# The last demodulation of a composed convolution moves from the weights to the rows that leave PSUM, and ScalarE makes the composition's first operand

## The chip, the core and the metric

The kernel runs on one core of a Trainium2 chip. The metric is the device time of one launch in microseconds (us): the median over runs. Below, PE is TensorE (matrix products), DVE is VectorE, ACT is ScalarE, POOL is GpSimd and SP is SyncE, whose queue issues most of the transfers. PSUM is the memory that TensorE writes its products to; SBUF is the working memory.

## The reference, cut to what matters

The input x has 32 samples of 64 channels and 1024 positions; every sample also has a condition vector of 128 numbers, its style. Two layers follow one another, and each adds its result to x:

```python
out = x
for l, typ in enumerate(('same', 'upsample', 'same', 'downsample')):
    s = style @ mod_w[l].T + mod_b[l]
    weight = SCALE * w[l] * s[:, None, :, None]
    demod = rsqrt(sum(weight * weight, axis=(2, 3)) + 1e-8)
    weight = weight * demod[:, :, None, None]     # one kernel per sample
    out = conv(out, weight, typ) + b[l]            # with a blur for up and down
...
x = x + ffn0(conv0(x))      # 64 experts of rank 16, the 16 best scores gated by softmax
x = x + ffn1(conv1(x))      # int4 weights, 1024 x 1024, and a bias
```

The two ffn parts act on the 1024 positions of one channel, so a row (sample, channel) is what they call a token. The demodulation of the fourth convolution is one number for each sample and output channel, that is, one number for each token.

## The kernel before

**Composition.** The four convolutions of a sample are linear and have no activation between them, so the kernel doesn't run them one by one. It runs the first convolution, and it multiplies the other three (with the blurs and strides) together into one small set of tap matrices for each sample, which TensorE then applies once to the first convolution's output. The work goes by pairs of samples: 16 pairs p in each of the layers i = 0 and 1, and a pair's 2 x 64 rows are the 128 partitions of everything that comes after.

- `composed1(i, p)` builds the operand `r` (L586): the fourth convolution's weights `w3p`, times a per-sample column `al2`, times the row of the fourth demodulation, `tbl[i, p][:, h, 0]`, broadcast over the partitions. One VectorE instruction for each of the two samples. TensorE multiplies `r` with `tw` into the product `g` (L596), and ScalarE takes it out of PSUM with a per-partition scale as `gs` (L608). There is one buffer for `r`.
- `composed2` makes `f` (L619) from `gs`, and `weights` copies it out (L634, L636, L637) and adds (POOL, L642, L648, L652): these are the tap matrices of `w(k)`.
- `first` is the first convolution (`c`, L757 or L768 and L773; ScalarE's copy out L758, or `yt` L770 and VectorE's L774 with a pointer scale). `differences_of` forms differences of its outputs (VectorE L716, POOL L722 and L730).
- `rest` applies the composed taps: products `r` in PSUM (L834, L843 or L852, L875), VectorE's sums (L865, L866, L883, L884), and in pairs that use nine products one more, `p`: ScalarE first copies the constant row of the fourth layer, `tbl[i, p][:, h, 1]`, into a PSUM bank (L822), TensorE adds `p` on it (L826), ScalarE copies it out as `rt` (L830). The result is then split into a high part (L149, `thx`) and a low part (L919, `tlx`) for the ffn products.
- `tbl` holds two rows a sample: row 0 is the demodulation, row 1 the constant that the biases make. `last_rows` makes them from two transposes per layer (L345, ScalarE's L346); for the first two pairs `spread_rows` broadcasts them by small matmuls (L355, copied by ScalarE in L364), for all others a DMA reads them from `rowd` (L571).
- `ends` computes the edge rows of all samples apart from the taps, layer by layer, with `scaled` (L464, L466), L482 and L483, L519 to L521, and products `ue`, `ve`, `re`.

**The ffn of layer 0.** `layer0` is its first half: score and expert products `h` (L955) in three chunks; `joined` takes them out of PSUM as `hs`. Pairs 0 and 1 (`WHOLE`) do it by a plain copy (L974). The others sum two banks: ScalarE scales the first (L976), VectorE adds the scaled second (L977). Then come the gates (L987 to L997, with ScalarE's `ga` L993), and POOL's gating (L1003). The gated rows are stored for all pairs; the second half, after the last pair, transposes them (`ht`, L1079) and forms the products `o` (L955), added to x in L1123 and L1124; meanwhile the factors of layer 1 (`factors`, L331 to L334 among them) and its first pairs are prepared.

**The ffn of layer 1** (`layer1`): products `q` (L1204) in three chunks; a column of `q` becomes `nrs` (L1223), VectorE forms `sc` from `q` and the weight scales (L1228) and adds with `nrs` (L1226), POOL adds it up (L1230). POOL also prepares the next pair's `o` with the bias (L1187, 128 x 1024).

**What sets the order.** Loop k of layer 0 handles pair k's ffn and, between its products, the next pairs' convolutions: `later(k + 1)` is `rest`, `conv(k + 2)` is `first`, `compose(k + 2)` is `composed1`, `weights(k + 2)` is `composed2`. The program records them in this order and a scheduler then arranges the instructions of each engine; every engine works its own list in order, and waits where an operand or a buffer is not ready. PSUM has eight banks: three for `c` and `r`, one for `g`, `f`, `p` and the small products, four for the ffn.

Of the kernel before, what the change touches and what calls it, by code (L numbers as in the profile page):

```python
# [15 lines left out]
P = 128  # L16
# [47 lines left out]
def adaln_ffn_kernel(ctx: ExitStack, tc: tile.TileContext, t, out: bass.AP):  # L64
# [44 lines left out]
    styp = const.tile([P, NP], F32, name="styp")  # L109
    rows = const.tile([B, 2, C], F32, name="rows")  # L110
    re = const.tile([P, 2, 2, P], F32, name="re")
# [6 lines left out]
    hgd = dram.tile([NP, P, L], F32, name="hgd")  # L118
    rowd = dram.tile([2, B, 2, C], F32, name="rowd")
    red = dram.tile([2, NP, 2, 2, 2, C], F32, name="red")  # L120
# [53 lines left out]
    def factors(i, *rooms):  # L174
# [20 lines left out]
        bi = tmp(NL)  # L195
        sty, dem, al, be = (tmp(NL, B) for _ in range(4))
        for h, hs in enumerate(halves):
# [78 lines left out]
        with tc.issue_after(done["positions"].ins if i == 0 else copied.ins):  # L276
            root = nc.scalar.activation(dem, dpv, AF.Sqrt, bias=eps, scale=0.5)
        v = nc.vector.reciprocal(dem, dem)
        with tc.issue_after(v.ins):
# [7 lines left out]
        with tc.issue_after(root.ins):  # L287
# [3 lines left out]
            nc.scalar.copy(tw[C:, 0, 1], w2v[C:, 0, C:])  # L291
        last_rows(i, 0, dem[:, 3])
        yield
# [16 lines left out]
        nc.vector.tensor_copy(al[:, 3], dem[:, 3])  # L310
        nc.vector.tensor_copy(be[:, 3], bib(3))
        nc.vector.tensor_copy(al2, al[:, 2])
# [15 lines left out]
        for l, src in ((2, be[:, 1]), (3, tm)):  # L328
            ps = mpst(f"cs{i}_{l}")[:, :B]
            for k in range(KT):  # L330
                nc.tensor.matmul(ps, cw[:, l, k], src, start=(k == 0), stop=(k == KT - 1))  # L331
            dst = tm if l == 2 else cst
            nc.vector.scalar_tensor_tensor(dst, ps, 8.0, al[:, l], ALU.mult, ALU.mult)
            nc.vector.tensor_tensor(dst, dst, be[:, l], ALU.add)  # L334
            if l == 2:
                yield
        last_rows(i, 1, cst)
        nc.sync.dma_start(rowd[i], rows)
        yield

    def last_rows(i, k, v):


        ps = mpst(f"rows{i}_{k}")
        nc.tensor.transpose(ps[:B, :C], v[:C], ident[:C, :C])  # L345
        nc.scalar.copy(rows[:, k], ps[:B, :C])  # L346
        if i == 0:
            spread_rows(0, k)

    def spread_rows(p, k):  # L350

        ps = fpst(f"rows{k}_{p}")[:, :P].rearrange("p (n c) -> p n c", n=2)
        for h in range(2):
            n = 2 * p + h
            nc.tensor.matmul(  # L355
                ps[:, h],
                ident[:B, n : n + 1].to_broadcast([B, P]),
                rows[:, k],
                start=True,
                stop=True,  # L360
            )
        if k == 0:
            tbl[0, p] = wk.tile([P, 2, 2, C], F32, tag="tbl", name=f"tbl0_{p}", bufs=3)
        nc.scalar.copy(tbl[0, p][:, :, k], ps)  # L364

# [83 lines left out]
    def ends(i, lo, hi, room, behind=()):  # L449
# [11 lines left out]
        def scaled(dst, ps, l):  # L461
            a = alp[:, l, lo:hi].unsqueeze(2).to_broadcast([P, n, dst.shape[2]])
            b = bep[:, l, lo:hi].unsqueeze(2).to_broadcast([P, n, dst.shape[2]])
            nc.vector.tensor_tensor(dst, ps, a, ALU.mult)  # L464
            by = nc.vector if l in (0, NL - 1) else eng
            done[f"s{l}"] = by.tensor_tensor(dst, dst, b, ALU.add)  # L466

# [101 lines left out]
    def tables(i, p):  # L569
        v = tbl[i, p] = wk.tile([P, 2, 2, C], F32, tag="tbl", name=f"tbl{i}_{p}", bufs=3)  # L570
        nc.sync.dma_start(  # L571
            v.rearrange("p a b c -> p (a b c)"),
            rowd[i, 2 * p : 2 * p + 2].rearrange("a b c -> (a b c)").partition_broadcast(P),
        )
# [6 lines left out]
    def composed1(i, p):  # L581

        r = wk.tile([P, 2, 2, C], F32, tag="r3", name=f"r3_{i}_{p}", bufs=1)
        for h in range(2):
            n = 2 * p + h
            nc.vector.scalar_tensor_tensor(  # L586
                r[:, :, h],
                w3p,
                al2[:, n : n + 1],
                tbl[i, p][:, h, 0].unsqueeze(1).to_broadcast([P, 2, C]),  # L590
                ALU.mult,
                ALU.mult,
            )
        ps = (fpst if i == 1 and p > 2 else mpst)(f"g{i}_{p}")
        for k in range(2):
            nc.tensor.matmul(  # L596
                ps[:, k * P : (k + 2) * P],
                tw[:, k].rearrange("p a b -> p (a b)"),
                r.rearrange("p a b c -> p (a b c)"),
                start=(k == 0),  # L600
                stop=(k == 1),
                skip_group_check=True,
            )
        g = wk.tile([P, 3, 2, C], F32, tag="g", name=f"gs{i}_{p}", bufs=1)
        v = ps[:, : 3 * P].rearrange("p (k h c) -> p k h c", k=3, h=2)
        for h in range(2):
            n = 2 * p + h
            nc.scalar.activation(g[:, :, h], v[:, :, h], AF.Copy, scale=al1[:, n : n + 1])  # L608
        return g
# [170 lines left out]
    def rest(i, n, y, f):  # L780
# [19 lines left out]
        if whole:  # L800
            yb, yo = y
            ps = cpst(f"r{i}_{n}")
            for j in range(4):
                for k in range(4):
# [8 lines left out]
                    )  # L813
            c = tbl[i, p][:, h, 1].unsqueeze(1).to_broadcast([P, 2 * 4, C])
            done["r0"] = nc.vector.tensor_tensor(th, shape(ps), c, ALU.add)
# [3 lines left out]
        if nine(i, p):  # L819
# [3 lines left out]
                pt.rearrange("p (q c) -> p q c", q=2),  # L823
                tbl[i, p][:, h, 1].unsqueeze(1).to_broadcast([P, 2, C]),
            )
# [36 lines left out]
        else:  # L862
            parts = [v.rearrange("p (q c) -> p q c", c=C) for v in (m, ps[:, 2 * P :])]
            common = tbl[i, p][:, h, 1].unsqueeze(1).to_broadcast([P, 4, C])
        done["m"] = nc.vector.tensor_tensor(*parts, common, ALU.add)  # L865
# [99 lines left out]
    def layer0(p, ws):  # L965
# [5 lines left out]
        def joined(col, w, qd):  # L971
            dst = hs[:, col : col + w]
            if whole:
                nc.scalar.copy(dst, qd[0])  # L974
                return
            nc.scalar.activation(dst, qd[0], AF.Copy, scale=1.0 + 1.0 / RADIX)  # L976
            nc.vector.scalar_tensor_tensor(dst, qd[1], -1.0 / RADIX, dst, ALU.mult, ALU.add)  # L977

# [215 lines left out]
    def layer1(p, wq, aux):  # L1194


        o = residual.pop(p)
        for c in range(3):
            if c == 0:
# [21 lines left out]
            if c == 0:  # L1221
                nrs = tiny.tile([P, 1], F32, tag="nrs", name=f"nrs{p}")
                nc.vector.tensor_scalar_mul(nrs, ps[:, 0:1], -1.0)  # L1223
            if c == (0 if p == NP - 1 else 2):
                with tc.issue_after(done["lo"].ins):
                    nc.vector.scalar_tensor_tensor(o, aux[:, 1], nrs, o, ALU.mult, ALU.add)  # L1226
            s = wk.tile([P, QC], F32, tag="yt", name=f"sc{p}_{c}", bufs=2)[:, : QC - a]
            nc.vector.tensor_tensor(s, ps[:, a:], aux[:, 0, cs], ALU.mult)  # L1228
            eng = nc.vector if p == NP - 1 and c == 2 else nc.gpsimd
# [101 lines left out]
    run(set0)  # L1331
    spread_rows(1, 0)
    for h in range(2):
# [4 lines left out]
    for h in range(2):  # L1338
        later(0, h)
    spread_rows(1, 1)  # L1340
    weights(1)
# [202 lines left out]
```

## Time and profile before

| | before |
|---|---|
| median of 3 runs | 893.91 us |
| lowest and highest | 893.53 and 894.51 us |
| span of the profiled execution | 893.1 us |
| PE busy | 866.1 us, 97% |
| DVE busy | 723.2 us, 81% |
| POOL busy | 531.1 us, 59% |
| ACT busy | 352.4 us, 39% |
| DMA | 109.81 MB, mean 123 GB/s |

The profile is one execution. Its span reaches from its first to its last instruction; the runs are timed around the launch, which is some 0.8 us more. In order of time: the start, then the taps and the products `h` of layer 0 for all 16 pairs (the last `h` at 397 us), then its products `o` (428.6 to 621.5), then the pairs of layer 1 (`q` from 621.9 to the end). A busy engine is not by that alone the one that sets the time: what matters is which engine the others wait for, and where.

### The profile page before, as it was taken

The numbers are of one execution on the slowest core, as the hardware profiler recorded it, in microseconds if no ns is written. First come the engines' busy times: TensorE is split into PE (matmuls) and PEld (weight loads), VectorE is DVE, ScalarE is ACT, GpSimd is POOL, SyncE is SP. The second block draws the span as 40 slices with busy tenths as digits, with TensorE's granted clock in tenths as the row PEclk, the third lists the DMA queues.
The fourth block names the chain that finished last, engine by engine and source line by source line (L and its number), as shares of the span: only waits on it lengthen the run. The fifth ranks groups of instructions, "written<-read, shape, count | busy, mean of one in ns | idle before, by whom it ended". The sixth has DMA issues, their size and how long they took to land.

```text
span 893.1 us, 14916 instructions
## 1 busy us (share of the span) xinstructions
PE 866.1 (97%) x5033; PEld 775.1 (87%) x5033; DVE 723.2 (81%) x1460; ACT 352.4 (39%) x817; POOL 531.1 (59%) x745
## 2 busy tenths in 40 slices
PE   6989999999999999999999999999999999999997
PEld 4876888999999999994688888888899999999997
DVE  4475898888888888778986765669999999999996
ACT  6444544444444444333332221247333433343340
POOL 7235654666666666556572222343787888888884
PEclk9999999999999999999999999999999999999999
DMA  8632222222232222345475666555543334334321
GB/s 240 155 73 54 54 69 62 88 89 80 79 91 83 81 79 71 106 178 149 139 232 193 201 193 197 189 192 167 164 117 111 98 100 143 114 90 139 122 66 71
DMA packets 49739, 109.81 MB, mean 123 GB/s; under 512 B 13700, under 2 KB 22400, under 8 KB 49664
## 3 DMA queue, kind: packets, MB, share of 16 engines
q1 hardware_dynamic: 48704, 107.88, 39.5%
q10 hardware_dynamic: 960, 0.99, 0.5%
q8 instruction: 40, 0.66, 0.3%
q14 instruction: 35, 0.29, 0.1%
HBM read 70.97 MB, written 37.88 MB: 122 GB/s over the span
## 4 chain that ended last, share of the span: by engine, by line
PE 42%; DVE 7%; POOL 2%; issue 2%; ACT 0%; DVEq 0%; POOLq 0%; ACTq 0%
PE o L955 16%; PE q L1204 11%; PE f L619 3%; PE r L875 3%; PE c L773 2%; PE r L834 1%; PE r L843 1%; PE c L768 1%; PE ht L1079 1%; PE g L596 1%; DVE cv L716 1%; DVE x L1124 1%; PE p L826 1%; DVE rt L866 1%; DVE r L884 0%
## 5 line engine op out<-in xcount | busy, mean ns | idle before, releaser
L716 DVE TENSOR_TENSOR cv<-cv 128x257 f32<-128x257 f32 x120 | 105.8, 913 | 1.3 <-ACT cv L758 0.9
L730 POOL TENSOR_TENSOR cv<-cv 128x256 f32<-128x256 f32 x120 | 77.7, 647 | 29.8 <-DVE cv L716 25.1
L722 POOL TENSOR_TENSOR cv<-cv 128x128 f32<-128x128 f32 x100 | 39.0, 411 | 67.5 <-PE r L843 48.3
L1204 PE MATMUL q<-wq,thx 128*128 128x342 f32 x384 | 73.0, 332 | 2.1 <-ACT thx L913 2.1
L955 PE MATMUL h<-wa,tdx 128*128 128x352 f32 (+1 forms) x336 | 72.2, 351 | 0.2 <-DVE wa L382 0.2
L1204 PE MATMUL q<-wq,tlx 128*128 128x342 f32 x384 | 72.3, 330 | 0.0
L619 PE MATMUL f<-gs,iw 128*128 128x128 f32 (+1 forms) x384 | 68.2, 327 | 0.1
L619 PEld LDWEIGHTS f<-gs,iw 128*128 128x128 f32 x384 | 61.8, 190 | 5.9 <-issue 0.5
L955 PE MATMUL h<-wa,thx 128*128 128x352 f32 (+1 forms) x336 | 64.7, 333 | 0.0
L1204 PEld LDWEIGHTS q<-wq,thx 128*128 128x128 f32 x384 | 60.3, 189 | 4.1 <-ACT thx L913 3.2
L770 ACT ACTIVATE yt<-c,be,al 128x257 f32<-128x257 f32 x56 | 31.7, 567 | 80.4 <-PE c L768 77.3
L875 PE MATMUL r<-cv 128*128 128x128 f32 x480 | 63.4, 274 | 0.0
L1204 PEld LDWEIGHTS q<-wq,tlx 128*128 128x128 f32 x384 | 61.9, 189 | 0.8
L955 PE MATMUL h<-wa,tlx 128*128 128x352 f32 (+1 forms) x336 | 62.4, 327 | 0.0
L955 PE MATMUL o<-wb,thh 128*128 128x512 f32 x224 | 60.4, 402 | 1.5 <-ACT wb L375 1.5
L935 POOL TENSOR_TENSOR tdx<-thx,tlx 128x1024 fp32r<-128x1024 f32 x14 | 34.7, 2479 | 44.5 <-ACT tlx L927 36.2
L955 PEld LDWEIGHTS h<-wa,tdx 128*128 128x128 f32 x336 | 56.9, 188 | 2.4 <-DVE wa L382 0.5
L1123 DVE SCALAR_TENSOR_TENSOR cv<-o,cv 128x512 f32<-128x512 f32 x26 | 18.0, 692 | 50.2 <-PE o L955 50.2
L955 PE MATMUL o<-wb,tlh 128*128 128x512 f32 x224 | 58.4, 397 | 0.0
L875 PEld LDWEIGHTS r<-cv 128*128 128x128 f32 x480 | 58.4, 191 | 0.0
L634 ACT COPY cv<-f 128x256 f32<-128x256 f32 x64 | 24.0, 375 | 83.9 <-PE f L619 46.3
L642 POOL TENSOR_TENSOR cv<-cv 128x256 f32<-128x256 f32 x60 | 50.0, 833 | 11.4 <-ACT cv L637 11.4
(313 smaller groups left out, 2274.6 us busy)
## 6 DMA issues: line engine op xcount, KB each, us to landing
cv<-in_x_dram SPq DMA_DIRECT2D x60, 256.0 KB
cv<-x1e SPq DMA_DIRECT2D x64, 192.5 KB
x1e<-dd SPq DMA_DIRECT2D x16, 514.0 KB
hgd<-hs SPq DMA_DIRECT2D x16, 512.0 KB
hg<-hgd SPq DMA_DIRECT2D x16, 512.0 KB
x1d<-x SPq DMA_DIRECT2D x16, 512.0 KB
xb<-x1d SPq DMA_DIRECT2D x16, 512.0 KB
out_dram<-o SPq DMA_DIRECT2D x15, 512.0 KB
```

Source lines behind the costliest of these rows:

```text
L619: done["f"] = nc.tensor.matmul(pv[:, n : n + 2 - k], iw[:, e].rearrange("p a b -> p (a b)"), v, start=(m == 0), stop=(m == len(steps) - 1) ...
L634: nc.scalar.copy(f8[:, 0::2], pv[:, :, h])
L642: nc.gpsimd.tensor_tensor(f[:, 4 * P : 6 * P].rearrange("p (a b) -> p a b", b=P), v[:, :, 0], v[:, :, 1], ALU.add,)
L716: nc.vector.tensor_tensor(d[:, k], yo[:, k : k + HQ], yb, ALU.subtract)
L722: nc.gpsimd.tensor_tensor(y[:, YB + k * P : YB + (k + 1) * P], y[:, 2 * k : 2 * k + 2 * P - 1 : 2], y[:, 1 : 2 * P : 2], ALU.subtract,)
L730: nc.gpsimd.tensor_tensor(e[:, :, k], d[:, :, 2 * k : 2 * k + HQ - 2 : 2], d[:, :, 1 : HQ - 1 : 2], ALU.subtract,)
L770: nc.scalar.activation(yt, mid, AF.Identity, bias=be0[:, n : n + 1], scale=a)
L875: done["r"] = nc.tensor.matmul(ps[:, j * P : (j + 1) * P], y[:, YE + (2 * q + k) * P : YE + (2 * q + k + 1) * P], w(q + 2 * k), start=True ...
L935: done["td"] = nc.gpsimd.tensor_tensor(*(v.rearrange("p a b -> p (a b)") for v in (td, *toks[key])), ALU.subtract)
L955: nc.tensor.matmul(banks[l == 2], toks[key][l][:, order(k)], w[:, cols], start=(k == first and l != 1), stop=(k == last and l in (2, min(n ...
L1123: nc.vector.scalar_tensor_tensor(v, qd[1], -SCALING / RADIX, v, ALU.mult, ALU.add)
L1204: nc.tensor.matmul(ps, half[:, k], wq[at(k)][:, c * QC : (c + 1) * QC], start=(k == 0 and j == 0), stop=(k == NC - 1 and j == 1),)
```

## The change

The fourth demodulation, `dem[:, 3]`, is no longer multiplied into the composed weights. Everything between the composition and the ffn products is computed without it, and the scale, a column `alp[:, 3, p]` with one number for each row of the pair, is applied where the ffn's products leave PSUM: in `joined` (as `outd`, which holds the two constants times it) and in `layer1` (`nrs` and `sc`). The constant that the biases make must be divided by the same number, so `be[:, 3]` becomes the bias times `roots`, the square root whose reciprocal is `dem`. The table then holds one row a sample instead of two, so one transpose and its spreading go, and the transferred table is half as large. `r` has only one per-partition scale left and becomes a ScalarE instruction.

```diff
         bi = tmp(NL)
-        sty, dem, al, be = (tmp(NL, B) for _ in range(4))
+        sty, dem, roots, al, be = (tmp(NL, B) for _ in range(5))
         for h, hs in enumerate(halves):
...
         with tc.issue_after(done["positions"].ins if i == 0 else copied.ins):
-            root = nc.scalar.activation(dem, dpv, AF.Sqrt, bias=eps, scale=0.5)
-        v = nc.vector.reciprocal(dem, dem)
+            root = nc.scalar.activation(roots, dpv, AF.Sqrt, bias=eps, scale=0.5)
+        v = nc.vector.reciprocal(dem, roots)
         with tc.issue_after(v.ins):
...
             nc.scalar.copy(tw[C:, 0, 1], w2v[C:, 0, C:])
-        last_rows(i, 0, dem[:, 3])
         yield
...
         nc.vector.tensor_copy(al[:, 3], dem[:, 3])
-        nc.vector.tensor_copy(be[:, 3], bib(3))
+        nc.vector.tensor_tensor(be[:, 3], roots[:, 3], bib(3), ALU.mult)
         nc.vector.tensor_copy(al2, al[:, 2])
...
                 nc.tensor.matmul(ps, cw[:, l, k], src, start=(k == 0), stop=(k == KT - 1))
-            dst = tm if l == 2 else cst
-            nc.vector.scalar_tensor_tensor(dst, ps, 8.0, al[:, l], ALU.mult, ALU.mult)
-            nc.vector.tensor_tensor(dst, dst, be[:, l], ALU.add)
             if l == 2:
+                nc.vector.scalar_tensor_tensor(tm, ps, 8.0, al[:, l], ALU.mult, ALU.mult)
+                nc.vector.tensor_tensor(tm, tm, be[:, l], ALU.add)
                 yield
-        last_rows(i, 1, cst)
+            else:
+                nc.vector.scalar_tensor_tensor(cst, ps, 8.0, be[:, l], ALU.mult, ALU.add)
+        if i == 0:
+            for k, f in enumerate((1.0 + 1.0 / RADIX, -1.0 / RADIX)):
+                nc.vector.tensor_scalar_mul(outd[:, k], alp[:, NL - 1], f)
+        last_rows(i, cst)
         nc.sync.dma_start(rowd[i], rows)
         yield

-    def last_rows(i, k, v):
-
-
-        ps = mpst(f"rows{i}_{k}")
+    def last_rows(i, v):
+
+
+        ps = mpst(f"rows{i}")
         nc.tensor.transpose(ps[:B, :C], v[:C], ident[:C, :C])
-        nc.scalar.copy(rows[:, k], ps[:B, :C])
+        nc.scalar.copy(rows, ps[:B, :C])
         if i == 0:
-            spread_rows(0, k)
-
-    def spread_rows(p, k):
-
-        ps = fpst(f"rows{k}_{p}")[:, :P].rearrange("p (n c) -> p n c", n=2)
+            spread_rows(0)
+
+    def spread_rows(p):
+
+        ps = fpst(f"rows{p}")[:, :P].rearrange("p (n c) -> p n c", n=2)
         for h in range(2):
             n = 2 * p + h
             nc.tensor.matmul(
                 ps[:, h],
                 ident[:B, n : n + 1].to_broadcast([B, P]),
-                rows[:, k],
+                rows,
                 start=True,
                 stop=True,
             )
-        if k == 0:
-            tbl[0, p] = wk.tile([P, 2, 2, C], F32, tag="tbl", name=f"tbl0_{p}", bufs=3)
-        nc.scalar.copy(tbl[0, p][:, :, k], ps)
+        tbl[0, p] = wk.tile([P, 2, C], F32, tag="tbl", name=f"tbl0_{p}", bufs=3)
+        nc.scalar.copy(tbl[0, p], ps)

...
             b = bep[:, l, lo:hi].unsqueeze(2).to_broadcast([P, n, dst.shape[2]])
-            nc.vector.tensor_tensor(dst, ps, a, ALU.mult)
+            if l < NL - 1:
+                nc.vector.tensor_tensor(dst, ps, a, ALU.mult)
+                ps = dst
             by = nc.vector if l in (0, NL - 1) else eng
-            done[f"s{l}"] = by.tensor_tensor(dst, dst, b, ALU.add)
+            done[f"s{l}"] = by.tensor_tensor(dst, ps, b, ALU.add)

...
     def tables(i, p):
-        v = tbl[i, p] = wk.tile([P, 2, 2, C], F32, tag="tbl", name=f"tbl{i}_{p}", bufs=3)
+        v = tbl[i, p] = wk.tile([P, 2, C], F32, tag="tbl", name=f"tbl{i}_{p}", bufs=3)
         nc.sync.dma_start(
-            v.rearrange("p a b c -> p (a b c)"),
-            rowd[i, 2 * p : 2 * p + 2].rearrange("a b c -> (a b c)").partition_broadcast(P),
+            v.rearrange("p a c -> p (a c)"),
+            rowd[i, 2 * p : 2 * p + 2].rearrange("a c -> (a c)").partition_broadcast(P),
         )
...
             n = 2 * p + h
-            nc.vector.scalar_tensor_tensor(
-                r[:, :, h],
-                w3p,
-                al2[:, n : n + 1],
-                tbl[i, p][:, h, 0].unsqueeze(1).to_broadcast([P, 2, C]),
-                ALU.mult,
-                ALU.mult,
-            )
+            nc.scalar.activation(r[:, :, h], w3p, AF.Copy, scale=al2[:, n : n + 1])
         ps = (fpst if i == 1 and p > 2 else mpst)(f"g{i}_{p}")
...
             if whole:
-                nc.scalar.copy(dst, qd[0])
+                nc.scalar.activation(dst, qd[0], AF.Copy, scale=alp[:, NL - 1, p : p + 1])
                 return
-            nc.scalar.activation(dst, qd[0], AF.Copy, scale=1.0 + 1.0 / RADIX)
-            nc.vector.scalar_tensor_tensor(dst, qd[1], -1.0 / RADIX, dst, ALU.mult, ALU.add)
+            nc.scalar.activation(dst, qd[0], AF.Copy, scale=outd[:, 0, p : p + 1])
+            nc.vector.scalar_tensor_tensor(
+                dst, qd[1], outd[:, 1, p : p + 1], dst, ALU.mult, ALU.add
+            )

...
         o = residual.pop(p)
+        scale = alp[:, NL - 1, p : p + 1]
         for c in range(3):
...
                 nrs = tiny.tile([P, 1], F32, tag="nrs", name=f"nrs{p}")
-                nc.vector.tensor_scalar_mul(nrs, ps[:, 0:1], -1.0)
+                nc.vector.tensor_scalar(nrs, ps[:, 0:1], -1.0, scale, ALU.mult, ALU.mult)
             if c == (0 if p == NP - 1 else 2):
                 with tc.issue_after(done["lo"].ins):
                     nc.vector.scalar_tensor_tensor(o, aux[:, 1], nrs, o, ALU.mult, ALU.add)
             s = wk.tile([P, QC], F32, tag="yt", name=f"sc{p}_{c}", bufs=2)[:, : QC - a]
-            nc.vector.tensor_tensor(s, ps[:, a:], aux[:, 0, cs], ALU.mult)
+            nc.vector.scalar_tensor_tensor(
+                s, ps[:, a:], scale, aux[:, 0, cs], ALU.mult, ALU.mult
+            )
             eng = nc.vector if p == NP - 1 and c == 2 else nc.gpsimd
...
     run(set0)
-    spread_rows(1, 0)
     for h in range(2):
...
         later(0, h)
-    spread_rows(1, 1)
+    spread_rows(1)
     weights(1)
```

The uses of `tbl` in `rest` change only their index. No other function is touched, and no loop order is written differently; `spread_rows(1, 0)` is left out, as its row no longer exists. In the built program ScalarE has 64 instructions `r` that VectorE had before.

More of the change, by code (lines that the diff above doesn't have):

```diff
@@ L109, in adaln_ffn_kernel @@
     styp = const.tile([P, NP], F32, name="styp")
-    rows = const.tile([B, 2, C], F32, name="rows")
+    rows = const.tile([B, C], F32, name="rows")
+    outd = const.tile([P, 2, NP], F32, name="outd")
     re = const.tile([P, 2, 2, P], F32, name="re")
@@ L118, in adaln_ffn_kernel @@
     hgd = dram.tile([NP, P, L], F32, name="hgd")
-    rowd = dram.tile([2, B, 2, C], F32, name="rowd")
+    rowd = dram.tile([2, B, C], F32, name="rowd")
     red = dram.tile([2, NP, 2, 2, 2, C], F32, name="red")
@@ L813, in rest @@
                     )
-            c = tbl[i, p][:, h, 1].unsqueeze(1).to_broadcast([P, 2 * 4, C])
+            c = tbl[i, p][:, h].unsqueeze(1).to_broadcast([P, 2 * 4, C])
             done["r0"] = nc.vector.tensor_tensor(th, shape(ps), c, ALU.add)
@@ L823, in rest @@
                 pt.rearrange("p (q c) -> p q c", q=2),
-                tbl[i, p][:, h, 1].unsqueeze(1).to_broadcast([P, 2, C]),
+                tbl[i, p][:, h].unsqueeze(1).to_broadcast([P, 2, C]),
             )
@@ L863, in rest @@
             parts = [v.rearrange("p (q c) -> p q c", c=C) for v in (m, ps[:, 2 * P :])]
-            common = tbl[i, p][:, h, 1].unsqueeze(1).to_broadcast([P, 4, C])
+            common = tbl[i, p][:, h].unsqueeze(1).to_broadcast([P, 4, C])
         done["m"] = nc.vector.tensor_tensor(*parts, common, ALU.add)
```

## Prediction

> **What bounds the kernel now.** I read the busy times of the page, then the table by stretches, then the groups of instructions with their shapes, then the waits of TensorE, then the rows in order of time around those waits. The page first:
>
> ```profile
> PE 866.1 (97%) x5033; PEld 775.1 (87%) x5033; DVE 723.2 (81%) x1460; ACT 352.4 (39%) x817; POOL 531.1 (59%) x745
> ```
>
> TensorE is idle for 27.0 of 893.1 us. The change takes no large matmul away, so all that it can win lies in those 27 us, and all that it can lose is new idle time. By stretches (window, its length, then the busy time of PE, PEld, DVE, ACT and POOL, each with its instructions; the clock; DMA):
>
> ```profile
> 0.00:40.00 40.00, 31.10 (x163) 26.07 (x163) 17.48 (x53) 19.92 (x49) 19.36 (x52) 1.00 0.82 217
> 160.00:400.00 240.00, 240.00 (x1510) 229.47 (x1510) 200.94 (x477) 107.26 (x246) 142.97 (x195) 1.00 0.29 89
> 600.00:720.00 120.00, 116.50 (x743) 108.23 (x742) 115.85 (x232) 50.60 (x123) 87.23 (x138) 1.00 0.44 135
> 720.00:868.00 148.00, 147.60 (x967) 141.88 (x965) 141.81 (x265) 59.87 (x156) 125.22 (x164) 1.00 0.38 113
> ```
>
> From 160 to 400 (layer 0 in its steady state) TensorE never stops: relief of VectorE is worth nothing there. From 600 to 720 VectorE works 115.85 of 120 us and TensorE loses 3.5: relief can count. From 720 to 868 TensorE loses 0.4. At the start 6.2 of 8.9 lost us are the wait for the first load, which stays. The waits of TensorE in single stretches (who waited for whom: us in all, times, longest) name the late engine:
>
> ```profile
> PE ve L535 <- DVE room L521: 1.2, 1, 1.2
> ...
> PE rows L345 <- DVE cv L334: 0.5, 1, 0.5
> ...
> PE c L773 <- DVE rt L866: 1.0, 2, 0.7
> PE q L1204 <- ACT thx L913: 0.7, 1, 0.7
> ```
>
> Nearly all are VectorE's. (The stalls priced below are the distance between the starts of two successive matmuls less the usual distance for the shape, read in order of time; they come out up to 0.4 us longer than these waits.) The groups give the prices (mean ns of one ahead of the last bar):
>
> ```profile
> L774 DVE SCALAR_TENSOR_TENSOR cv<-c,al,yt 128x257 f32<-128x257 f32 x56 | 26.5, 474 | 0.7 <-ACT yt L770 0.7
> L586 DVE SCALAR_TENSOR_TENSOR r<-w3p,al,tbl 128x128 f32<-128x128 f32 x64 | 25.8, 414 | 3.0 <-ACT tbl L364 2.6
> L608 ACT ACTIVATE gs<-g,al 128x192 f32<-128x192 f32 x64 | 24.4, 415 | 4.0 <-PE g L596 3.2
> L865 DVE TENSOR_TENSOR rt<-r,rt 128x256 f32<-128x256 f32 x50 | 20.8, 415 | 32.2 <-PE r L843 32.2
> L976 ACT ACTIVATE hs<-h 128x368 f32<-128x368 f32 x28 | 13.4, 477 | 80.0 <-PE h L955 80.0
> ```
>
> **The change, part by part.** *Unit prices.* VectorE loses 64 r products, 25.8 us. They cost 324 ns where nothing disturbs them and up to 1243. A product with a pointer scale (L774) takes 59 ns more than the plain one of its width (L865, 474 against 415), so the 48 sc products, now with a pointer, add 48 x 0.06 = 2.9 us; the 42 joining products (L977, 531 ns) go from an immediate to a pointer, 0 to 0.06 each. ScalarE gains 64 r products. No row shows a 128x128 ACTIVATE with a pointer from SBUF; the plain copy of that shape (L822) takes 270 ns and L608, half as wide again, 415, so 0.27 to 0.415; I take 0.36, nearer to L608, which has the pointer. L701 (128x384, pointer) takes 612 ns where L976 (128x368, immediate) takes 477: the 48 scalings of hs get up to 0.12 longer. The Trainium skill (ScalarE: Activation LUTs, Rules for kernel authors) says to use VectorE and not ScalarE for a multiplication; in this trace the two prices are nearly equal, and what decides is who stands in the queue. The sum goes by these rows.
>
> *1. Start, 10 to 45 us.* The first demodulated row, its transpose and half of the small spreading matmuls disappear; the first composition no longer waits for the table. TensorE waited 0.6 us for ACT L346 at 15.74, 0.46 for r at 19.75, 0.6 for L334 at 29.59. Against it two r products now stand on ScalarE ahead of the copy at 16.49 (L758) until al2 is there (17.4): that copy ends 1.6 us later, but the bank that it frees is next needed at 20.55. I take half of the 1.66, -0.8; bounds -1.3, and +1.0 should the copies of the first convolution come late.
>
> *2. 52.01 and 59.85.* Ahead of the 1.2 us wait of ve VectorE runs two r products in one chain (50.35 and 51.21, 0.26 us from one start to the next instruction's). Without them and with the shorter row work ahead, -0.6; at 59.85 the g product waits 0.65 for a bank that L464 frees, in the same chain, -0.5. Sum -1.1; bounds 0 and -1.6.
>
> *3. hs with a pointer, pairs 0 and 1* (82 and 110 us, where TensorE waits anyway): +0.2, 0 to +0.3.
>
> *4. Layer 0, nine pairs: the term that speaks against.* In the changed order of ScalarE one r product stands between the second gs and the copy p of the odd sample (gs, ga, gs, r, p, r, rt), from p_11 to p_27. Before, in order of time (start, us, engine, line):
>
> ```profile
> 250.57 0.42 ACT L608 ACTIVATE gs<-g,al 128x192 f32<-128x192 f32 x1
> ...
> 250.89 0.34 ACT L993 ACTIVATE ga<-hs,su 128x64 f32<-128x64 f32 x1
> ...
> 251.12 0.41 ACT L608 ACTIVATE gs<-g,al 128x192 f32<-128x192 f32 x1
> ...
> 251.57 0.27 ACT L822 COPY p<-tbl 128x128 f32<-128x128 f32 x1
> ...
> 251.91 0.32 PEld L826 LDWEIGHTS p<-cv 128*128 128x128 f32 x2
> 251.94 0.48 PE L826 MATMUL p<-cv 128*128 128x128 f32 x2
> ```
>
> The copy ends at 251.84 and its matmul starts 0.10 later. In six of the nine pairs the distance is this same 0.10, in three 0.13: as good as no slack. But neighbours on ScalarE overlap: ga starts 0.32 after a gs of 0.42. The copy itself waits for the gs before it to end (251.53), as it fills the bank that gs reads. So r can start at 251.42, in that wait, and the copy 0.25 after it at 251.67, not at 251.57: 0.10 us of TensorE per pair, 9 x 0.10 = +0.9. Without overlap it is 0.41 - 0.04 = 0.37 each, +3.3; with a shorter r +0.3. The even sample's copy is 2.4 us early, those of layer 1 two or more; there r stands ahead of a copy (L830) before which ScalarE is idle over 1 us. Nothing in those places.
>
> *5. 496.43.* The row's transpose waits 0.5 (a stall of 0.77) behind L333 and L334, which become one instruction with one sum less: -0.7; bounds -0.5 and -0.75.
>
> *6. 600 to 704.* Here r is on the path. Four rows:
>
> ```profile
> 627.79 0.96 DVE L586 SCALAR_TENSOR_TENSOR r<-w3p,al,tbl 128x128 f32<-128x128 f32 x2
> 628.67 2.88 DVE L482 TENSOR_TENSOR room<-xg,styp 128x24 f32<-128x24 f32 x1
> ...
> 628.57 2.94 POOL L1187 TENSOR_TENSOR o<-xb,aux 128x1024 f32<-128x1024 f32 x1
> ...
> 632.19 0.71 PE L834 MATMUL r<-cv 128*128 128x128 f32 x4 [0.30 <-DVE cv L774]
> ```
>
> A product of 24 columns takes 2.88 us: it started 0.1 after POOL's wide one and ended with it (631.5). Its twin L483 takes 0.17. Without the two r's L482 starts at 627.8 and is done before POOL begins; L774 then runs when its yt is there (630.2, not 631.6), and the stalls at 632.19 (0.46) and 642.12 (1.09), one VectorE chain with no gap, can go. The Trainium skill (SBUF — State Buffer, Who interferes with whom) has this as a rule: a VectorE instruction with two SBUF inputs and a GpSimd one that reads SBUF exclude each other, and the first to start wins. By that rule r itself (w3p and the table) was such an instruction, and leaves. The other stalls: 602.40 (0.32; r at 593.28 lies in the chain ahead), 684.81 (0.49) and 703.49 (0.88; both behind chains with two r's, some 0.9 and 0.7, less two pointers at 0.06). All five: 0.3 + 0.46 + 1.09 + 0.49 + 0.7 = 3.0. 610.67 and 620.32 have no r ahead of them and stay. What is late next is POOL's wide product, which holds whichever VectorE instruction meets it: I take three quarters, -2.2; bounds -0.8 and -3.4.
>
> *7. 704 to the end.* Each pair frees VectorE 0.83 - 0.23 us, hidden by TensorE. The last sc products stand on the closing chain: +0.1, to +0.3. The halved tables (DMA of 64 instead of 128 KB a pair) were never waited for. The outd scales are two instructions at the start: nothing.
>
> Sum: -0.8 - 1.1 + 0.2 + 0.9 - 0.7 - 2.2 + 0.1 = -3.6. The profiled span is 893.1 and the median of the runs 893.9, 0.8 around it: a span of 889.5, a time of 890.3. All best ends together give about 887, all worst ones about 897.
>
> **Rivals.** (a) *ScalarE does not overlap*: the copy p is late by 0.37 in each of nine pairs, +2.4 on the sum: 892.7. For it: copies that follow one another on ScalarE show no overlap (242.05 to 242.34). Against: ACTIVATEs do. (b) *VectorE's relief is absorbed*: the held instruction only becomes another, term 6 gives -0.8 and term 2 -0.5: 892.3, and with (a) beside it 894.7. (c) *Slower: POOL's wide product lands worse.* In layer 1 each of the ten steady pairs after 704 has one (2.9 us); VectorE idles there 6.2 of 148 us, 0.6 a pair, and gets 0.6 more. Shifted earlier, VectorE may meet it with an instruction that TensorE needs. It decides if the hold exceeds these 1.2 us; half of 2.9 less that is 0.3, and up to twice that, on ten pairs +3 to +6; with 0.6 the time is 890.3 + 6 = 896.3. Against: TensorE loses only 0.4 there today with a hold in every pair. (d) *All five stalls and the start go*, and r hides in the wait: 888.
>
> **How the numbers follow.** The forecast 0.52 (its own range 888.7 to 891.9), (a) or (b) alone 0.20, (c), or (a) and (b) with a late start, 0.20, (d) 0.08. The range 888.0 to 895.2 leaves out the best end and most of (c). A measurement can tell about 0.2%, 1.8 us: faster is below 892.1, which takes the forecast, (d) and a little of (b): 0.62. Within 0.2%: 0.19. Slower: 0.19.
>
> **What would show it.** Right: the p matmuls of the odd samples start 0.1 later behind the second gs in nine layer-0 pairs; L482's successor takes 0.2; the waits for L866 near 685 and 703 are gone; VectorE's busy time is near 723.2 - 25.8 + 2.9 + 1 = 701, ScalarE's near 352 + 23 + 4 = 379. Wrong: TensorE loses 0.3 or more in each of those nine pairs, or a new multi-microsecond VectorE row sits ahead of a TensorE wait after 600.

## The result and the profile after

The changed kernel takes 896.47 us (median of 9 runs, 895.58 to 897.98) against 894.11 us. By these medians it is slower by 2.4 us, where 3.6 less were forecast; the ratio on record is 1.0022, 95% interval 1.0013 to 1.0031. The profiled execution has a span of 896.1 us, 3.0 more than before; it is the slowest of the nine, 897.98 us. (Every run with a span on record took 1.7 to 1.9 us more than that span, not the 0.8 said ahead of the prediction.) Ratios are of fast runs alone; one run of e3 below, the profiled one, was slow, with 1451 us at a granted clock of 0.56. From the page:

```profile
PE 866.8 (97%) x5023; PEld 775.4 (87%) x5023; DVE 698.3 (78%) x1393; ACT 374.6 (42%) x877; POOL 530.2 (59%) x745
```

VectorE lost 25 us and ScalarE gained 22, close to the 701 and 379 forecast for them, and the time went up. The table by stretches (columns as before) shows where:

```profile
0.00:40.00 40.00, 29.92 (x146) 26.33 (x147) 16.10 (x48) 21.20 (x52) 19.09 (x52) 0.91 0.81 215
160.00:400.00 240.00, 237.78 (x1474) 223.92 (x1474) 187.99 (x448) 110.37 (x255) 138.25 (x192) 1.00 0.28 86
600.00:720.00 120.00, 118.68 (x750) 110.60 (x749) 111.18 (x218) 57.72 (x145) 90.00 (x140) 1.00 0.43 135
720.00:868.00 148.00, 148.00 (x979) 142.87 (x978) 137.61 (x252) 62.95 (x166) 125.53 (x164) 1.00 0.37 114
```

Layer 0 from 160 to 400, where TensorE never stopped, now does 1474 of its former 1510 matmuls in the same 240 us. The first 40 us have a mean clock of 0.91. Layer 1 is better: 118.68 of 120 us busy instead of 116.50. The distance between the same matmul in both traces gives the account:

| stretch (us of before) | late at its end | change |
|---|---|---|
| to 59.85, g of pair 1 | +0.97 | +1.0 |
| to 158.0, first p of layer 0 | +0.57 | -0.4 |
| to 353.3, the tenth even p | +6.32 | +5.75 |
| to 600.1, o | +5.27 | -1.05 |
| to 719.9, q | +2.40 | -2.9 |
| to 868.0, q | +2.29 | -0.1 |
| end of the span | +3.0 | +0.7 |

From 400 to 460 two things cancel: the kernel before had a mean clock of 0.96 from 400 to 440, the changed one 1.00, but a new wait of 1.1 us for VectorE's L1123 at 451.6.

**Layer 0.** The waits of TensorE from 160 to 400 have a new line, which the kernel before did not have at all:

```profile
PE p L824 <- POOL cv L650: 1.8, 9, 0.2
```

The p of the even sample waits for POOL's sums of the tap matrices. In order of time around one of these waits, after:

```profile
241.28 2.64 POOL L933 TENSOR_TENSOR tdx<-thx,tlx 128x1024 fp32r<-128x1024 f32 x1 [3.06 <-ACT tlx L925]
...
241.64 2.90 DVE L714 TENSOR_TENSOR cv<-cv 128x257 f32<-128x257 f32 x2
...
244.46 0.59 DVE L975 SCALAR_TENSOR_TENSOR hs<-h,outd,hs 128x368 f32<-128x368 f32 x1
...
245.13 1.14 POOL L1003 TENSOR_TENSOR hs<-hs,ga 128x368 f32<-128x368 f32 x1 [1.21 <-DVE hs L975]
...
247.62 0.46 POOL L650 TENSOR_TENSOR cv<-cv 128x128 f32<-128x128 f32 x1
...
248.13 0.50 PE L824 MATMUL p<-cv 128*128 128x128 f32 x2 [0.21 <-POOL cv L650]
```

and before, one pair of the same kind:

```profile
238.27 0.54 DVE L977 SCALAR_TENSOR_TENSOR hs<-h,hs 128x368 f32<-128x368 f32 x1
238.72 2.95 DVE L716 TENSOR_TENSOR cv<-cv 128x257 f32<-128x257 f32 x2
...
238.89 2.50 POOL L935 TENSOR_TENSOR tdx<-thx,tlx 128x1024 fp32r<-128x1024 f32 x1 [3.58 <-ACT tlx L927]
...
241.35 1.00 POOL L1003 TENSOR_TENSOR hs<-hs,ga 128x368 f32<-128x368 f32 x1
```

VectorE's two differences (elsewhere 0.76 us for both) take 2.9 us in both kernels, since they meet POOL's wide product and end only behind it; below this is called a hold. Before, the joining sum of the third chunk stood ahead of them. In the changed program it stands behind: it waits out the hold, POOL's gating waits for it, the sums wait for the gating, and p for the sums. The period of a pair is 22.3 instead of 21.7 us.

**Start.** The first g waits for r, and the clock falls (the row of TensorE's waits, then windows of 4 us):

```profile
PE g L594 <- ACT r L591: 2.1, 1, 2.1
```

```profile
14.00:18.00 4.00, 2.33 (x8) 1.60 (x6) 4.00 (x11) 2.33 (x6) 3.82 (x5) 1.00 1.02 304
18.00:22.00 4.00, 3.52 (x9) 2.88 (x10) 1.52 (x11) 3.80 (x9) 1.15 (x4) 0.61 1.06 379
```

This g starts at 18.48 us, 1.3 us earlier than before (19.75), so the wait alone is not a loss against the kernel before. The time goes with the clock, which falls a second time, from 32.52 to 35.92 us, behind no such wait. The row of that stretch, then the same one in e11 below, whose order up to there is the same:

```profile
32.52:35.92 3.40, 3.40 (x13) 2.97 (x12) 0.00 (x0) 1.42 (x5) 0.00 (x0) 0.50 0.84 183
32.40:35.80 3.40, 3.40 (x26) 3.23 (x26) 0.15 (x1) 1.58 (x5) 0.00 (x0) 1.00 0.79 181
```

From the first c to the g of pair 1 the kernel before needs 48.0 us, this execution with two falls 49.1, e11 with one 47.5, and e4, which has the same order up to the first g and none, 46.7. So, by this comparison, about 2.4 us of this one execution are lost clock, and at full clock the changed start is 1.3 us faster than the one before.

**End.** The masked copy of the last sample starts 0.01 us behind POOL's addition and takes 1.22 us; before it started 0.04 ahead of it and took 0.43. ScalarE's thx, and with it the last products q, come late. After, then before:

```profile
881.29 0.94 POOL L1233 TENSOR_TENSOR o<-o,sc 128x342 f32<-128x342 f32 x1
881.30 1.22 DVE L882 COPY_PREDICATED r<-ident,re 128x256 f32<-128x256 int32 x1
```

```profile
878.96 0.43 DVE L884 COPY_PREDICATED r<-ident,re 128x256 f32<-128x256 int32 x1
879.00 1.16 POOL L1230 TENSOR_TENSOR o<-o,sc 128x342 f32<-128x342 f32 x1
```

**Layer 1** did what was forecast: the product that POOL held for 2.88 us is done before POOL begins.

```profile
632.46 0.18 DVE L487 TENSOR_TENSOR room<-xg,styp 128x24 f32<-128x24 f32 x1
...
633.17 2.89 POOL L1187 TENSOR_TENSOR o<-xb,aux 128x1024 f32<-128x1024 f32 x1
```

### The profile page after: what moved, and what is told of

Its sections match the earlier page's. It is cut to its first block, busy times and chain, and to the rows that moved or that the text cites. A ratio compares the mean times of both kernels' runs of the same rounds, so it can differ in the third digit from the quotient of the medians.

```text
span 896.1 us, 14882 instructions
## 1 busy us (share of the span) xinstructions
PE 866.8 (97%) x5023; PEld 775.4 (87%) x5023; DVE 698.3 (78%) x1393; ACT 374.6 (42%) x877; POOL 530.2 (59%) x745
## 4 chain that ended last, share of the span: by engine, by line
PE 43%; DVE 5%; POOL 2%; issue 1%; ACT 0%; DVEq 0%; POOLq 0%
PE o L953 14%; PE q L1205 12%; PE f L617 3%; PE r L873 3%; PE c L771 3%; PE r L832 1%; PE g L594 1%; PE c L766 1%; PE r L841 1%; PE ht L1079 1%; PE p L824 1%; POOL wb L377 1%; DVE nib L437 1%; DVE r L882 1%; DVE r L881 0%
## 5 line engine op out<-in xcount | busy, mean ns | idle before, releaser
L714 DVE TENSOR_TENSOR cv<-cv 128x257 f32<-128x257 f32 x120 | 104.0, 897 | 1.5 <-ACT cv L756 1.0
L728 POOL TENSOR_TENSOR cv<-cv 128x256 f32<-128x256 f32 x120 | 77.4, 645 | 29.3 <-DVE cv L714 24.6
L1003 POOL TENSOR_TENSOR hs<-hs,ga 128x368 f32<-128x368 f32 (+1 forms) x48 | 43.6, 922 | 24.7 <-DVE hs L975 11.8
L974 ACT ACTIVATE hs<-h,outd 128x368 f32<-128x368 f32 (+1 forms) x42 | 23.6, 563 | 82.5 <-PE h L953 82.1
L1123 DVE SCALAR_TENSOR_TENSOR cv<-o,cv 128x512 f32<-128x512 f32 x26 | 18.0, 691 | 50.1 <-PE o L953 50.0
```

What stands on the lines that cost most here:

```text
L714: nc.vector.tensor_tensor(d[:, k], yo[:, k : k + HQ], yb, ALU.subtract)
L728: nc.gpsimd.tensor_tensor(e[:, :, k], d[:, :, 2 * k : 2 * k + HQ - 2 : 2], d[:, :, 1 : HQ - 1 : 2], ALU.subtract,)
L1003: nc.gpsimd.tensor_tensor(v, v, g, ALU.mult)
```

## The experiments

The theory: r's leaving VectorE turned VectorE's order in layer 0 round, and this, with r ahead of the odd samples' copy on ScalarE, is the whole loss of 5.75 us; the start and the end have causes of their own. The rivals: the pointer scales of the joining, or r's place on ScalarE alone. Times are medians, ratios are against runs of the kernel before on the same chip. What the traces lose against the kernel before in layer 0, from the first to the tenth even p (158.0 to 353.3 us of before), decides between them:

| kernel | order of VectorE | r | lost, us |
|---|---|---|---|
| changed | differences first | ScalarE | 5.75 |
| e1 | joining sum first | VectorE | 0.40 |
| e2 | differences first | ScalarE, behind the copy p | 5.63 |
| e3 (trace of e11) | joining sum first | ScalarE | 1.53 |
| e4 | joining sum first | ScalarE, behind the copy p | 0.12 |

**e1: r back on VectorE**, without the table.

```diff
-            nc.scalar.activation(r[:, :, h], w3p, AF.Copy, scale=al2[:, n : n + 1])
+            nc.vector.tensor_scalar_mul(r[:, :, h], w3p, al2[:, n : n + 1])
```

> The changed kernel with the 64 products r back on VectorE, as a product with one pointer scale and without the table; all else as changed. Theory (order): the layer-0 loss of 5.8 us comes from r having left VectorE, whose list then has two differences ahead of the joining sum of the third chunk, and from r ahead of the copy p on ScalarE. Both are undone: a period of 21.7 us per pair from 160 to 380 instead of 22.3, TensorE 240 of 240 us busy from 160 to 400, no wait of p for POOL; layer 1 gives back up to 2.5 of its 2.9 us. Time 890.5 to 893. Rival (price): the pointer scales of the joining make layer 0 slow; they stay here, so the period stays near 22.3 and the time is 895 to 897.

Measured 896.98 us, ratio 1.0024 (1.0015 to 1.0033): the time is the rival's, the mechanism the theory's. The pointers are all still there, layer 0 is whole again, and on VectorE the joining sum stands ahead of the differences:

```profile
160.00:400.00 240.00, 240.00 (x1510) 229.32 (x1509) 199.13 (x476) 107.82 (x243) 143.65 (x197) 1.00 0.29 89
```

```profile
240.03 0.60 DVE L975 SCALAR_TENSOR_TENSOR hs<-h,outd,hs 128x368 f32<-128x368 f32 x1
240.54 2.95 DVE L714 TENSOR_TENSOR cv<-cv 128x257 f32<-128x257 f32 x2
```

So neither the pointer scales nor the table make layer 0 slow: it is r's absence from VectorE. The gain was eaten elsewhere. From 600 to 720 us e1 wins 0.6 us on the kernel before instead of 2.9, as the stalls at 684.8 and 703.5 came back (1.4 us). And the start is worse, as r now stands on VectorE behind its small steps:

```profile
PE g L594 <- DVE r L591: 4.2, 1, 4.2
```

TensorE's clock is 0.50 from 17.2 to 24.0 us in this trace. The expectation says nothing of the start; it did not price that the small products that used to keep TensorE busy there were gone too.

**e2: r of layer 0 out of the way of the odd copy** (ScalarE), VectorE as changed.

```diff
+            with tc.issue_after(done["pc"].ins) if i == 0 and p > 6 else nullcontext():
-            nc.scalar.activation(r[:, :, h], w3p, AF.Copy, scale=al2[:, n : n + 1])
+                nc.scalar.activation(r[:, :, h], w3p, AF.Copy, scale=al2[:, n : n + 1])
...
-            nc.scalar.copy(
+            done["pc"] = nc.scalar.copy(
                 pt.rearrange("p (q c) -> p q c", q=2),
```

> The changed kernel with r of layer 0 (from pair 7 on) queued on ScalarE behind the copy p of an even sample, out of the way of the odd sample's copy; VectorE's order stays as changed. Theory (two stalls, each with its own cause): the odd samples' p no longer starts 0.16 us late in nine pairs, the even ones' 0.36 remains: 1.5 us less, 895.0. Rival (one stall only, that of the even sample, sets the period): no change, 896.5. If ScalarE's queue were the whole cause: 5.8 less, 890.7.

Measured 896.99 us, ratio 1.0025 (1.0015 to 1.0035). The odd p is in time, and nothing is won: the even p waits longer instead.

```profile
PE p L825 <- POOL cv L651: 3.2, 9, 0.4
```

Its period stays at 22.3 us. The loop through VectorE's hold and POOL's sums sets it, and the odd stall lay inside that loop.

**e3: the joining sum first.** The differences of the odd samples are recorded behind the joining sum and queued after it; r stays on ScalarE.

```diff
+            done["join"] = nc.vector.scalar_tensor_tensor(
...
+        if i == 0 and n % 2 and nine(i, n // 2):
+            late.append(firsts)      # the two differences
...
+        while late:
+            with tc.issue_after(done["join"].ins):
+                late.pop(0)()
```

> The changed kernel with the differences of the odd samples of layer 0 queued on VectorE behind the joining sum of the third chunk, r left on ScalarE. Theory: POOL's gating, its sums and the even samples' p come in time again; ten times 0.36 = 3.6 us less, 892.9, and the odd samples' 0.16 stays. Rival (the pointer price of joining, or r's place on ScalarE, is the cause): less than 1 us changes.

Measured 891.75 us, the median of four, ratio 0.9968 (0.9955 to 0.9981): a larger gain than forecast. Its trace is read in e11.

**e4: both.**

> Both orders mended, r left on ScalarE. Theory: the two stalls add up, 5.1 to 5.8 us less, TensorE again 240 of 240 us busy from 160 to 400, 890.7 to 891.4, below the kernel before (894.1) by what layer 1 gained less the losses at the start and the end. Rival (the stalls hide each other): as the better of the two alone, 892.9.

Measured 892.04 us, ratio 0.9969 (0.9957 to 0.9981): from 1.0022 to 0.9969 is 0.53%, 4.7 us, short of the 5.1 to 5.8 forecast, though layer 0 alone gives back 5.6. In the profiled run TensorE is busy from 160 to 400, and layer 1 keeps most of its gain:

```profile
160.00:400.00 240.00, 239.80 (x1502) 228.59 (x1501) 195.25 (x458) 115.21 (x265) 144.49 (x193) 1.00 0.29 89
600.00:720.00 120.00, 118.11 (x767) 111.37 (x766) 112.47 (x226) 56.93 (x141) 88.75 (x141) 1.00 0.41 131
```

**e11: e3 once more, for its trace.**

> The kernel of e3 once more, for its trace: VectorE's order mended, r still ahead of the copy p of the odd samples. Theory (term 4 of the prediction as it was priced, 0.1 to 0.16 us for each of nine pairs): a period of 21.8 to 21.86 us per pair. Rival (the delay is made up, as another wait sets the period): 21.70.

The single run took 892.59 us. The period is 21.84 us, as forecast: the even p no longer waits, the odd one starts 0.16 late in nine pairs, 1.4 us against e4. Here is the term that the prediction priced, seen by itself:

```profile
250.87 0.41 ACT L606 ACTIVATE gs<-g,al 128x192 f32<-128x192 f32 x1
251.17 0.40 ACT L591 ACTIVATE r<-w3p,al 128x128 f32<-128x128 f32 x1
...
251.47 0.27 ACT L826 COPY p<-tbl 128x128 f32<-128x128 f32 x1
...
251.84 0.48 PE L830 MATMUL p<-cv 128*128 128x128 f32 x2
```

r starts inside the end of gs, as argued, and the copy follows 0.30 after it and not 0.25. The times of e3 and e4 do not show this difference. Their runs spread over 1.0 and 2.1 us, which can hide it; that is an argument and was not measured.

**e5: al2 early.** On e4.

```diff
+        nc.vector.scalar_tensor_tensor(al2, dem[:, 2], 0.125, sty[:, 3], ALU.mult, ALU.mult)
         nc.scalar.copy(al0, al[:, 0])
...
-        nc.vector.tensor_copy(al2, al[:, 2])
```

> On the kernel with both orders mended (892.0): the column al2 is written directly, right after the first scales, instead of copied at the end of VectorE's row of small steps. Theory (start): TensorE idles 2.0 us before its first g because r on ScalarE waits for al2 and the copies of the first convolution stand behind it; the idle time then often costs clock. With r at 16.2 instead of 17.8 the idle time is below 0.6 and the clock near 1.00 in every run: 1.5 to 2 us less, 890.0 to 890.5. Rival (the clock at the start depends on the first load, or on nothing in the program): at most 0.5 less.

Measured 889.75 us, ratio 0.9939 (0.9926 to 0.9952), a little more than forecast. TensorE waits 0.9 us for its first r instead of 1.8, and the g of pair 1 comes 45.0 us after the first c instead of 46.7, with the clock at 1.00 in both traces: the gain there is the shorter wait itself. The clock near 1.00 in every run did not come: three of the five runs have a mean of 0.997, and they spread over 2.1 us, as e4's do.

**e6: the first composition behind the first convolutions.** On e4.

```diff
-    compose(0)
     for h in range(2):
         conv(0, h)
+    compose(0)
```

> On the kernel with both orders mended (892.0): the first composition is recorded behind the first convolutions, so that on ScalarE two copies of c stand ahead of r, and on TensorE the fourth c product ahead of g. Theory (start, head of the queue): TensorE has a product to run while al2 is made, idles at most 1.2 us there and keeps its clock: 1 to 2 us less, 890.0 to 891.0. Rival (g is later, and all that follows from it): 0 to 1 us more.

Measured 889.73 us, ratio 0.9940 (0.9926 to 0.9954). Two copies of c now stand ahead of r, the fourth c runs while al2 is made, and g hardly waits:

```profile
16.31 1.02 ACT L763 ACTIVATE cv<-c,be,al 128x257 f32<-128x257 f32 x2
16.93 0.70 PE L761 MATMUL c<-cv,c 128*128 128x256 f32 x2 [0.86 <-ACT cv L763]
...
17.52 0.69 ACT L592 ACTIVATE r<-w3p,al 128x128 f32<-128x128 f32 x2 [0.19 <-DVE al L312]
...
18.27 0.91 PE L595 MATMUL g<-r,tw 128*128 128x256 f32 x3 [0.21 <-ACT r L592]
```

The g of pair 1 comes 45.2 us after the first c. Two unlike edits that shorten TensorE's wait win 1.7 and 1.4 us by then in their traces. The times say less: e4 ran on another chip, and e7, next, which leaves the start as it is in e4, took 890.11 us on the chip of e5 and e6, only 0.4 us more and within the intervals.

**e7: an sc product at the end moved, the wrong one.** On e4.

```diff
+        done["taps"] = nc.vector.tensor_tensor(ps, ps, both[:, :H], ALU.add)
...
+            late_sc = p == NP - 2 and c == 2
+            with tc.issue_after(done["taps"].ins) if late_sc else nullcontext():
```

> On the kernel with both orders mended (892.0): the last sc product of pair 14 is queued on VectorE behind the sum of the last sample's taps, so that the masked copy of its edge rows starts before POOL's addition and is not held by it (1.22 us instead of 0.43 in the changed kernel, where it started 0.01 us behind that addition). Theory (who starts first): 0.8 us less at the end, 891.2. Rival (the end is set by POOL's chain): no change, 892.0.

Measured 890.11 us, ratio 0.9949 (0.9936 to 0.9961). The trace shows the end as it was, the masked copy at 1.22 us: the product ahead of the sums was the middle chunk's.

```profile
873.38 1.22 DVE L889 COPY_PREDICATED r<-ident,re 128x256 f32<-128x256 int32 x1
873.38 0.92 POOL L1242 TENSOR_TENSOR o<-o,sc 128x342 f32<-128x342 f32 x1
```

The time nevertheless came out lower than e4's on another chip. The two traces show no gain of the edit: e7 is 0.4 us ahead of e4 from the first c on and stays so up to 875 us. What lowered the times on this chip stays open.

**e8: e4, e6 and e7 together.**

> Both orders mended, the first composition behind the first convolutions, and the end's sc product moved: the sum of e4, e6 and e7. Theory: 889.0 to 890.2, TensorE idle less than 25 us. Rival (the gains at start and end are not there): 892.0.

Measured 888.77 us, ratio 0.9930 (0.9918 to 0.9943), a little below the forecast, with the end as in e7. From the first c to 868 us its trace wins the same 7.0 us on the kernel before as e6's, and the end is as in e6 too. So the 1.0 us between the medians of e6 and e8 shows how little one such difference proves.

**e9: the right one.** On e6, the middle sc of pair 14 and its addition come behind the last sample's low part.

```diff
+            if p == NP - 2 and c == 1:
+                held_back = added        # the sc product and its addition
+            else:
+                if p == NP - 2 and c == 2:
+                    with tc.issue_after(done["lo"].ins):
+                        held_back()
+                added()
```

> The kernel of e6 with the middle sc product of pair 14 and its addition on POOL moved behind the last sample's low part, so that the sums of that sample come 0.48 us earlier and its masked copy meets POOL's wide product at its end, before the next addition. (In e7 it was the wrong sc product that was moved: the middle one stands ahead of these sums.) Theory (who starts first): the copy takes 0.43 instead of 1.22 us, the high part and TensorE's last q products come 1.2 us earlier: 888.5 to 889.0. Rival (POOL's additions end the kernel): 889.7 or more.

Measured 887.85 us, ratio 0.9923 (0.9910 to 0.9937). The copy now meets only the end of POOL's wide product (869.34 + 2.91 = 872.25) and is done at 872.54. From 868 us to TensorE's end e9 loses nothing against the kernel before, e6 0.8 us:

```profile
869.34 2.91 POOL L1194 TENSOR_TENSOR o<-xb,aux 128x1024 f32<-128x1024 f32 x1
...
871.97 0.57 DVE L889 COPY_PREDICATED r<-ident,re 128x256 f32<-128x256 int32 x1
```

**e10: e9 with al2 early.**

> The kernel of e9 with al2 written early as well. Theory (g still waits 0.3 to 0.4 us for r in e6): 0.3 to 0.5 less than e9, 888.2 to 888.5. Rival (c sets the start by then): the same as e9.

Measured 887.59 us, ratio 0.9922 (0.9908 to 0.9935), not to be told from e9 by the times. In its trace g no longer waits for r, and the g of pair 1 comes 0.4 us earlier after the first c, but TensorE now waits 0.6 us for the copy of c. This kernel beats both: 7.0 us below the kernel before, 9 below the changed one by the ratios. Its runs lie within 0.4 us; those of the changed kernel spread over 2.4.

## Why the prediction was wrong

**The step that failed is the reading of layer 0**: "relief of VectorE is worth nothing there", and term 4 as the only term that speaks against. The stretch was priced at +0.9 us and lost 5.75. Both took VectorE's order in layer 0 as given. ScalarE's new order was read line by line, VectorE's was not, though the part ahead of the prediction says that a scheduler makes all of them. With r gone it puts the differences ahead of the joining sum. e1 shows that r's absence brings this order, e3 and e11 that this order costs the time; why the scheduler prefers it was not tried. Rival (c), the slower one, had the right mechanism, a VectorE instruction held by POOL's wide product with something behind it that TensorE needs, but placed it in layer 1 after 704, where nothing was lost. The prediction's own sign of being wrong, 0.3 us or more lost in each of nine pairs, came (0.6 a pair), but by way of VectorE and not of term 4.

**Term 4** was right in place and low in size: 0.16 a pair (e11) against 0.10, 1.4 against 0.9 us, as r takes 397 ns and not 360. In the changed kernel it costs nothing of its own (e2).

**Term 1** was forecast at -0.8 with +1.0 as its worst end, should the copies of the first convolution come late, and the profiled execution lost 1.3 us up to 50 us. The copies did come late, but the loss is lost clock, which the sum had no term for: the same order at full clock (e4) gains 1.0 us up to there. "The bank that it frees is next needed at 20.55" was read from the order of before. Without the transposes and spreading products TensorE was through with its first three c outputs by 16.3. Next in its order stood g, whose r waited for al2 until 17.7; with c in its place (e6), TensorE waited for that bank until 16.9. Rows that are taken away may have been cover. That the profiled execution was hit by two falls of the clock is chance: e11 had one, and the fastest of the nine runs were 2.4 us shorter.

**Term 2**: -0.3 instead of -1.1. The chain of small VectorE steps ahead of ve is still 1.0 us late without r.

**Term 3** was not seen: from 60 to 158 us the kernel gained 0.4.

**Terms 5 and 6** held: 496.43 gave 0.67 where 0.7 was said, 600 to 720 gave 2.9 where 2.2 was said. Not each stall gave its part: 642.12 gave 0.4 of its 1.09 and 602.40 nothing, while 0.4 came unforecast between 610 and 630. L482 did what was forecast, the waits at 684.8 and 703.5 are gone. The small prices held too: sc 568 ns (+60), the scaling of hs 567 (+90), the joining 587 (+56).

**Term 7**: the sc price of 0.06 us was right and its effect not. +0.1 became +0.7, since these 0.06 us decided which of two engines started first.

## What to carry to other kernels

Where a scheduler or a planner makes the order, work taken off an engine is a change of that engine's order: compare the order of every engine that loses work, not only of the one that gains it, and follow what each overtaken instruction feeds. Shared holds between VectorE and POOL make such swaps cost microseconds instead of tenths, so look first at what now stands behind an instruction that is held. When an instruction moves to another queue, ask what it waits for and which PSUM bank the instructions behind it were about to free.

## What the runs showed of the hardware

- **The hold is decided by who comes first, to 0.05 us.** The masked copy took 0.43 us when it started 0.04 ahead of POOL's addition and 1.22 us when it started 0.01 behind it; L482 and its successor took 2.88 and 0.18. The Trainium skill (SBUF — State Buffer, Who interferes with whom) says that whichever of the two issues first gets the shared ports for its whole instruction, and both pairs agree with it. Where both start in the same hundredth of a microsecond (e4 and e7) the copy was held as well, for 1.21 and 1.22 us, so such a tie can't be read from the start times.
- **TensorE's clock at the start is partly a matter of chance.** With a wait of 2.1 us ahead of g the changed kernel fell to 0.61 in the four microseconds after, e11 with 2.2 to 0.59; e2 with 2.1 and e7 with 2.8 us stayed at 1.00, e1 with 4.2 fell to 0.50. A fall at the start lasts 3.41 us (18.85 to 22.26), in e1 twice that. In the 3.41 us ahead of it TensorE was busy for 1.26 us in the changed kernel (15.44 to 18.85) and for 1.22 in e11; e7's wait lies across two such stretches (13.70 to 17.11 to 20.53) with 1.60 and 2.38 us. That could be the reason for the difference, but it is not shown: the fall at 32.52 came behind 2.94 busy of 3.40 us, and e11 with the same 2.94 had none. The Trainium skill (TensorE: Matmul & The Clock Gate, What's actually happening) has a free-running window of about 3.4 us for it: that agrees with a loss that comes in some executions and not in others. That no idle stretch below a whole window should cost clock does not agree: 2.1 us sufficed. Whether a shorter wait keeps the clock up is not shown either: e5 and e6 have one and are at 1.00 there in their traces, but so are e4 and e7 without it.
- **Neighbouring ScalarE instructions overlap** by about 0.11 us (gs and r, 250.87 to 251.17 for an instruction of 0.41), unless the second waits for the first.
